# Rotating k before q, and v in 8 KB runs, in an attention and mixture-of-experts kernel

## The chip, the cores and the metric

The kernel runs on one core of one Trainium2 chip, in one launch. Its time is the time on the device, in microseconds (us); the median of several executions counts. One more execution was taken with the hardware profiler, and all stretches and durations below are from that one. The engines of the core are TensorE (PE in the profile; PEld are its weight loads), VectorE (DVE), ScalarE (ACT), GpSimd (POOL), and SyncE (SP), which here only issues DMAs.

## The reference

One transformer layer with the norm behind each half, all in fp32: x is 4 x 1024 x 256, attention has 16 heads of 64 with a rotary embedding and a causal mask, and the second half is a mixture of 16 experts of which each token takes 3.

```
proj = x @ W_in.T + b_in                   # q, k, v: 16 heads x 64 each
q, k = rope(q, sin, cos), rope(k, sin, cos)
att = softmax(mask(q @ k.T / 8)); y = att @ v
x = layernorm(x + y @ W_out.T + b_out)
raw = softmax(x @ gate); top 3 of 16, made to sum to 1
hidden = relu(x @ W1[e] + b1[e]); out = hidden @ W2[e] + b2[e]
x = layernorm(x + sum over the chosen e of gate_e * out_e)

def rope(x):                               # hi: first 32 of a head's 64, lo: last 32
    return concat(lo * cos + hi * sin, hi * cos - lo * sin)
```

## The kernel before, in words

**Tiling.** Attention goes over pairs of heads: 8 pairs for each of 4 sequences, n = 0 to 31. A pair has six slots (k = 0 to 5). Each slot takes one or two chunks of 128 queries, the longest first: chunk 7 (1024 keys by the causal mask), 6, 5, 4, then (3, 2), then (1, 0). A tile has 128 partitions: two heads by 64.

**What happens to a chunk.** `scores` (L254) multiplies q by k on TensorE into PSUM (L275), DVE adds the mask, keeps the row's extreme and writes the result to SBUF (L283), ACT makes the exponential and its row sum (L295). `divide` (L306) takes the reciprocal of the sum on DVE (L309) and multiplies each head's rows by it on POOL (L312). Two slots later `turn` (L321) transposes the divided rows in 32 x 32 blocks on DVE (L333), and `product` (L343) multiplies v by them on TensorE (L357). `close` adds the bias of v on ACT (L370), and `out` (L376) multiplies by the output weights on TensorE (L379) and adds the result to the residual on DVE (L384).

**Projection of the next pair.** In slots 0 to 3 of pair n, `project(n + 1, i, g)` (L193) makes q (i = 0) and k (i = 1) of the next pair: TensorE multiplies one half of 512 positions (L200), ACT adds the bias (L204). i = k // 2 and g = k % 2, so q is made in slots 0 and 1 and k in slots 2 and 3. After the second half, four DMAs copy the result with blocks of 32 partitions swapped into a tile `swp` (L213).

**Rotation.** `rotate` (L215) multiplies the projection by the sine in place, the swapped copy by the cosine, and adds them. The first product waits until the swap DMAs have read the projection. q (in slot 3): the sine on DVE (L217), the cosine (L221) and the sum (L222) on POOL. k (in slot 4): all three on POOL. For the first pair the engines differ. The first scores of a pair need its q and its k rotated: that is the seam between two pairs.

**v.** `values` (L224) projects 256 positions of v for two pairs at a time, in slots 4 and 5: TensorE (L231), ACT (L236), and one DMA to DRAM (L239). `spread` (L245) brings v back, 512 positions at a time, four times over (each time into 32 partitions): partition q holds positions 32 k + q for k = 0 to 15, so a run in DRAM is one position of one pair, 128 floats (L250). It is called in slot 1 (second half) and in slot 4 (first half).

**What sets the order.** TensorE's instructions stand in the order in which the program is written. The others are placed by a scheduler, which keeps the ties made by `after` (an instruction is issued behind the last one of a kind, with no semaphore) and by `late` (SP's DMAs keep program order). `turn` is tied behind the slot's scores, the reciprocals behind the turns. L384 is tied to nothing; the scheduler puts it inside the turns in slot 3 and behind the reciprocals in slots 0, 4 and 5.

**Routing.** Once a sequence is done, its layer norm and the choice of experts run within the next sequence's pairs: the norm in the slot 1 of its second pair, transposes and gate products up to the third pair, the choice (some 60 small DVE operations) in slot 3 of the third, the placing in slot 3 of the fourth, and 24 indirect DMAs issued by POOL that write a table (L641), four each in slots 1 and 3 of the fifth to seventh pairs. After the last pair the experts run (L830, L846, L860), which the change doesn't touch.

Of the kernel before, what the change touches and what calls it, by code (L numbers as in the profile page):

```python
# [37 lines left out]
P = 128  # L38
# [49 lines left out]
def attention(  # L88
# [5 lines left out]
    with ExitStack() as ctx:  # L94
# [98 lines left out]
        def project(n, i, g):  # L193

            b, p = divmod(n, NP)
            if g == 0:
                rot[n, i] = qkp.tile([P, T], FP, tag=f"rot{i}", name=f"rot{i}")
            ps = ps_s.tile([P, 512], FP, tag="s", name="pp")
            for c in range(DC):
                nc.tensor.matmul(  # L200
                    ps, lhsT=wqk[n][:, c, i, :], rhs=xts[b, g][:, c, :],
                    start=(c == 0), stop=(c == DC - 1),
                )
            nc.scalar.activation(  # L204
                rot[n, i][:, ts(g, 512)], ps, AF.Identity,
                bias=(bq_s if i == 0 else bqk[:, 1, :])[:, p : p + 1],
                scale=SCALE if i == 0 else 1.0,
            )
            if g == 1:

                swp = swps[n, i] = qkp.tile([P, T], FP, tag="swp", name="swp")
                for r in range(4):
                    nc.sync.dma_start(out=swp[ts(r, 32), :], in_=rot[n, i][ts(r ^ 1, 32), :])  # L213

        def rotate(n, i):  # L215
            swp, res = swps.pop((n, i)), rot[n, i]
            first = (nc.gpsimd if i and n else nc.vector).tensor_tensor(res, res, sin, ALU.mult)  # L217
            if n and i == 0:
                after(first, "turn" if "turn" in order else "scores")
            eng = nc.vector if n == 0 and i else nc.gpsimd  # L220
            eng.tensor_tensor(swp, swp, cos, ALU.mult)  # L221
            eng.tensor_tensor(res, res, swp, ALU.add)  # L222

        def values(n, cc):  # L224

            b = n // NP
            v = vp.tile([P, 2, 2 * P], FP, tag="v", name="v")
            ps = ps_s.tile([P, 2, 2 * P], FP, tag="s", name="vv")
            for u in range(2):
                for c in range(DC):  # L230
# [4 lines left out]
                    )  # L235
            nc.scalar.copy(v, ps)  # L236
            if cc == 0:
                vds[n // 2] = v_d.tile([T, 2 * P], FP, tag="v_d", name="v_d")
            nc.sync.dma_start(  # L239
                out=vds[n // 2][ts(cc, 2 * P)].rearrange("(u p) d -> p u d", p=P), in_=v  # L240
            )

        vds, vrs = {}, {}

        def spread(n, g):  # L245

            vr = vrs[n, g] = vrp.tile([P, 16, P], FP, tag=f"v{g}", name="vr")
            src = vds[n // 2][ts(g, 512), ts(n % 2, P)].rearrange("(k q) d -> q k d", q=32)
            for a in range(4):
                late(nc.sync.dma_start(out=vr[ts(a, 32)], in_=src))  # L250

# [54 lines left out]
        def divide(n, ends, kind):  # L306
            for qc, rsum in ends:
                rinv = sp.tile([P, 2], FP, tag="rinv", name="rinv")
                after(nc.vector.reciprocal(rinv, rsum), kind)  # L309
                for hh in range(2):  # L310
                    pr = probs[n, qc, hh]
                    router.behind = nc.gpsimd.tensor_scalar(  # L312
                        pr, pr, rinv[:, hh : hh + 1], 1.0, ALU.mult, ALU.mult
# [6 lines left out]

        def turn(n, i, kind):  # L321
            if n not in turned:
# [3 lines left out]
                )  # L326
            for hh in range(2):
                pr = probs.pop((n, i, hh))
                for h, (t, step) in enumerate(zip(turned[n], (7, 3))):
                    n_j = min(4, i + 1 - 4 * h)  # L330
                    if n_j <= 0:
                        continue
                    order["turn"] = router.on_dve = nc.vector.transpose(  # L333
                        t[:, hh, :, ds(i - 4 * h, n_j, step=step), :],
                        pr[:, ds(512 * h, n_j * P)].rearrange(
                            "p (j u q) -> p u j q", u=4, q=32
                        ),
                    )
                    after(order["turn"], kind)

        st = {}

        def product(n, j):  # L343
# [32 lines left out]
        def out(n, h):  # L376
            ps = ps_s.tile([P, 2, D], FP, tag="s", name="oo")
            for v in range(2):
# [29 lines left out]
        with tc.manual_schedule(engines={mybir.EngineType.PE}):  # L408
            for n in range(n_pairs + 2):
# [3 lines left out]
                for k in range(n_slots):  # L413
# [7 lines left out]
                    if k != 2 and one_of(m):  # L421
                        for j in js:
                            product(m, j)
                    if k in (0, 3, 4, 5) and one_of(n - 1 - (k == 0)):
                        out(n - 1 - (k == 0), (k - 3) % 4 if k else 3)
# [624 lines left out]
```

## Time and profile before

| | |
|---|---|
| median of 6 runs | 2107.82 us (2106.53 to 2110.24) |
| the profiled execution | 2109.6 us |
| its span, first to last instruction | 2107.7 us |
| attention, to the last pair's start | 1489.75 us, 31 seams |
| a pair without routing work | 42.4 to 44.0 us |
| a pair with scatters | 53.0 to 56.9 us |
| PE busy | 1751.2 us (83%) |
| POOL busy | 1223.7 us (58%) |
| DVE busy | 1148.9 us (55%) |
| granted TensorE clock | 0.900 of full speed |
| HBM read, written | 193.28 MB, 54.63 MB |

How to read it: the shares of busy time are means over attention and experts. A line of a timeline is: start in us from the span's start, duration, engine, line of the kernel, operation, tiles written and read, sizes, count, and in brackets how long the engine was idle just before and what ended that. `x8` at TensorE counts passes: an fp32 product takes two. "issue" is time in which an engine waited for nothing that the profile shows.

### The profile page before, as it was taken

The numbers are of one execution on the slowest core, as the hardware profiler recorded it, in microseconds if no ns is written. First come the engines' busy times: TensorE is split into PE (matmuls) and PEld (weight loads), VectorE is DVE, ScalarE is ACT, GpSimd is POOL, SyncE is SP. The second block draws the span as 40 slices with busy tenths as digits, with TensorE's granted clock in tenths as the row PEclk, the third lists the DMA queues.
The fourth block names the chain that finished last, engine by engine and source line by source line (L and its number), as shares of the span: only waits on it lengthen the run. The fifth ranks groups of instructions, "written<-read, shape, count | busy, mean of one in ns | idle before, by whom it ended". The sixth has DMA issues, their size and how long they took to land.

```text
span 2107.7 us, 52088 instructions
## 1 busy us (share of the span) xinstructions
PE 1751.2 (83%) x21172; PEld 1194.6 (57%) x21172; DVE 1148.9 (55%) x3453; ACT 724.6 (34%) x1662; POOL 1223.7 (58%) x1037
## 2 busy tenths in 40 slices
PE   7788887898877788887778897877589799999990
PEld 4455554555544455554445565543368588888880
DVE  5566665768755566875555768755445122222224
ACT  4344443444333344443234443333222122222223
POOL 4655565555665565456565564555536677777743
PEclk9889998999988998998889998988689699999995
DMA  6445454563444556354334554333357588888857
GB/s 180 103 122 126 89 117 105 102 174 79 105 88 84 96 122 164 85 120 89 79 86 103 153 117 92 82 72 75 65 212 207 131 227 240 232 237 238 233 129 249
DMA packets 239106, 284.86 MB, mean 135 GB/s; under 512 B 20897, under 2 KB 204321, under 8 KB 230802
## 3 DMA queue, kind: packets, MB, share of 16 engines
q1 hardware_dynamic: 211378, 248.18, 46.3%
q0 software_dynamic: 27344, 33.35, 8.9%
q8 instruction: 166, 2.72, 0.6%
q14 instruction: 74, 0.61, 0.1%
q10 hardware_dynamic: 144, 0.01, 0.0%
HBM read 193.28 MB, written 54.63 MB: 118 GB/s over the span
## 4 chain that ended last, share of the span: by engine, by line
PE 55%; DVE 16%; POOL 14%; issue 8%; DMA 3%; ACT 2%; SPq 1%; another core or an unknown queue 1%; ACTq 0%; POOLq 0%; DVEq 0%
PE y_ps L357 13%; PE ps L830 11%; PE ps L846 11%; PE s L275 10%; PE pp L200 7%; POOL rot L222 4%; DVE p L283 4%; DVE t_first L333 3%; POOL swp L221 3%; POOL p L312 3%; POOL rot L217 3%; DVE t_last L333 3%; PE oo L379 2%; POOL table L641 2%; PE ps L818 1%
## 5 line engine op out<-in xcount | busy, mean ns | idle before, releaser
L312 POOL TENSOR_SCALAR p<-p,rinv 128x512 f32<-128x512 f32 (+7 forms) x512 | 402.2, 800 | 492.5 <-DVE rinv L309 488.5
L295 ACT ACTIVATE p<-p,nmax 128x512 f32<-128x512 f32 (+7 forms) x512 | 392.0, 766 | 651.6 <-DVE nmax L283 592.5
L275 PE MATMUL s<-rot,rot 64*128 64x512 f32 (+3 forms) x1536 | 383.7, 590 | 213.8 <-POOL rot L222 187.0
L283 DVE CUSTOM_DVE_ANT_0 p<-s,zero 128x512 f32<-128x512 f32 x256 | 166.2, 685 | 467.4 <-PE s L275 448.8
L275 PEld LDWEIGHTS s<-rot,rot 64*128 64x128 f32 x1536 | 167.5, 209 | 423.3 <-POOL rot L222 197.3
L333 DVE STREAM_TRANSPOSE t_first<-p 128x512 f32<-128x512 f32 (+3 forms) x512 | 283.9, 583 | 0.0
L200 PE MATMUL pp<-xT,wqk 128*128 128x512 f32 x512 | 254.0, 621 | 20.4 <-DVE nmax L283 14.8
L357 PE MATMUL y_ps<-t_first,vr 32*64 32x160 f32 (+2 forms) x8192 | 233.6, 344 | 14.5 <-issue 12.5
L830 PE MATMUL ps<-xg,w 128*128 128x256 f32 x1008 | 236.8, 388 | 7.4 <-issue 3.7
L860 POOL DMA_INDIRECT sums<-y,ids x126 | 200.8, 1593 | 71.0 <-DVE y L856 36.3
L846 PE MATMUL ps<-w,hid 128*128 128x256 f32 x1008 | 234.7, 385 | 7.6 <-issue 7.2
L835 ACT ACTIVATE hid<-ps,w 128x256 f32<-128x256 f32 x252 | 105.4, 470 | 373.7 <-issue 305.6
L851 DVE TENSOR_TENSOR y<-ps,w 128x512 f32<-128x512 f32 x63 | 43.6, 691 | 344.4 <-PE ps L846 286.3
L221 POOL TENSOR_TENSOR swp<-swp,cos 128x1024 f32<-128x1024 f32 x63 | 150.3, 2385 | 137.6 <-DMA swp<-rot 136.3
L357 PEld LDWEIGHTS y_ps<-t_first,vr 32*64 32x64 f32 x8192 | 175.3, 132 | 84.1 <-issue 56.7
L846 PEld LDWEIGHTS ps<-w,hid 128*128 128x128 f32 x1008 | 193.4, 192 | 38.6 <-issue 13.4
L830 PEld LDWEIGHTS ps<-xg,w 128*128 128x128 f32 x1008 | 191.6, 195 | 34.5 <-issue 6.9
L357 PEld LDWEIGHTS y_ps<-t_last,vr 32*64 32x64 f32 x7424 | 123.0, 147 | 106.1 <-issue 60.4
L357 PE MATMUL y_ps<-t_last,vr 32*64 32x96 f32 (+3 forms) x7424 | 150.9, 274 | 34.0 <-DVE t_last L333 27.3
L200 PEld LDWEIGHTS pp<-xT,wqk 128*128 128x128 f32 x512 | 94.5, 195 | 113.0 <-issue 67.0
L379 PE MATMUL oo<-wo,yT 128*128 128x256 f32 x512 | 153.0, 425 | 2.6 <-ACT yT L370 1.7
L222 POOL TENSOR_TENSOR rot<-rot,swp 128x1024 f32<-128x1024 f32 x63 | 149.6, 2374 | 2.5
(146 smaller groups left out, 1914.8 us busy)
## 6 DMA issues: line engine op xcount, KB each, us to landing
w<-in_wall_dram SPq DMA_DIRECT2D x63, 1154.0 KB
vr<-v_d SPq DMA_DIRECT2D x256, 256.0 KB
swp<-rot SPq DMA_DIRECT2D x256, 128.0 KB
v_d<-v SPq DMA_DIRECT2D x64, 256.0 KB
wqk<-in_w_qk_dram SPq DMA_DIRECT2D x32, 256.0 KB
xT<-in_xT_dram SPq DMA_DIRECT2D x8, 512.0 KB
wv<-in_w_v_dram SPq DMA_DIRECT2D x16, 256.0 KB
wo<-in_w_outT_dram SPq DMA_DIRECT2D x32, 128.0 KB
```

What stands on the lines that cost most here:

```text
L200: nc.tensor.matmul(ps, lhsT=wqk[n][:, c, i, :], rhs=xts[b, g][:, c, :], start=(c == 0), stop=(c == DC - 1),)
L221: eng.tensor_tensor(swp, swp, cos, ALU.mult)
L222: eng.tensor_tensor(res, res, swp, ALU.add)
L275: nc.tensor.matmul(s[:, :n_k], lhsT=q[ts(hh, KD), ts(qc, P)], rhs=k[ts(hh, KD), ds(k0, n_k)], start=True, stop=True,)
L283: order["scores"] = nc.vector.tensor_tensor_reduce(out=probs[n, qc, hh][:, ds(k0, n_k)], in0=s[:, :n_k], in1=mask[:, 512 - n_k :] if last ...
L295: nc.scalar.activation(pr, pr, AF.Exp, bias=m, scale=-1.0, accum_out=rsum[:, hh : hh + 1])
L312: router.behind = nc.gpsimd.tensor_scalar(pr, pr, rinv[:, hh : hh + 1], 1.0, ALU.mult, ALU.mult)
L333: order["turn"] = router.on_dve = nc.vector.transpose(t[:, hh, :, ds(i - 4 * h, n_j, step=step), :], pr[:, ds(512 * h, n_j * P)].rearrange ...
L357: nc.tensor.matmul(st[n][a][ts(hh, KD), ds(32 * j, 32 * (TC - j))], lhsT=vrs[n, h][ts(a, 32), jh * 4 + u, ts(hh, KD)], rhs=t[ts(a, 32), hh ...
L830: nc.tensor.matmul(ps[:, f - f0, :], lhsT=w[:, ds(c * FF + f * P, P)], rhs=xg[:, c, :], start=(c == 0), stop=(c == DC - 1),)
L846: nc.tensor.matmul(ps[:, h, :], lhsT=hid[:, f, ts(h, P)], rhs=w[:, ds(W2_AT + f * D, D)], start=(f == 0), stop=(f == FC - 1),)
L860: s = nc.gpsimd.indirect_dma_start(out=sums[t % 2], out_offset=bass.IndirectOffsetOnAxis(ap=ids[:, h, i : i + 1], axis=0), in_=y[:, h, :], ...
```

## The change

It has three parts.

- **k first.** Slots 0 and 1 now project k, slots 2 and 3 project q (second half first). k is rotated in slot 2 and q in slot 4. Rotations are tied behind the last division (`order["divide"]`) for what POOL does; q's sine product on DVE stays tied behind the last turn.
- **v in DRAM.** The DRAM tile is laid out so that what one partition of `vr` reads is one run of 8 KB. Each `values` stores its two pairs with two DMAs, whose DRAM side has the dimensions 4 x 32 x 256. `product` takes v's rows at other places in the tile.
- **Sums between the turns.** `out` returns what is to be added, and the slot's loop does the sum (was L384) between the turns of the two heads; the reciprocal stands behind them.

```diff
         def project(n, i, g):
             b, p = divmod(n, NP)
-            if g == 0:
+            half_done = (n, i) in rot
+            if not half_done:
                 rot[n, i] = qkp.tile([P, T], FP, tag=f"rot{i}", name=f"rot{i}")
...
-            if g == 1:
+            if half_done:
                 swp = swps[n, i] = qkp.tile([P, T], FP, tag="swp", name="swp")
...
         def rotate(n, i):
             swp, res = swps.pop((n, i)), rot[n, i]
             first = (nc.gpsimd if i and n else nc.vector).tensor_tensor(res, res, sin, ALU.mult)
-            if n and i == 0:
-                after(first, "turn" if "turn" in order else "scores")
+            if n:
+                after(first, "divide" if i else "turn" if "turn" in order else "scores")
             eng = nc.vector if n == 0 and i else nc.gpsimd
-            eng.tensor_tensor(swp, swp, cos, ALU.mult)
+            second = eng.tensor_tensor(swp, swp, cos, ALU.mult)
+            if n:
+                after(second, "divide")
             eng.tensor_tensor(res, res, swp, ALU.add)
...
-            v = vp.tile([P, 2, 2 * P], FP, tag="v", name="v")
+            v = vp.tile([P, 2, 2, P], FP, tag="v", name="v")
...
-            nc.scalar.copy(v, ps)
+            nc.scalar.copy(v.rearrange("p i u d -> p u i d"), ps.rearrange("p u (i d) -> p u i d", i=2))
             if cc == 0:
-                vds[n // 2] = v_d.tile([T, 2 * P], FP, tag="v_d", name="v_d")
-            nc.sync.dma_start(
-                out=vds[n // 2][ts(cc, 2 * P)].rearrange("(u p) d -> p u d", p=P), in_=v
-            )
+                vds[n // 2] = v_d.tile([NG, 2, 32, 2, 4, 2 * P], FP, tag="v_d", name="v_d")
+            for i in range(2):
+                nc.sync.dma_start(
+                    out=vds[n // 2][cc // 2, i, :, cc % 2].rearrange("q k d -> k q d"),
+                    in_=v[:, i],
+                )
...
-            src = vds[n // 2][ts(g, 512), ts(n % 2, P)].rearrange("(k q) d -> q k d", q=32)
             for a in range(4):
-                late(nc.sync.dma_start(out=vr[ts(a, 32)], in_=src))
+                late(nc.sync.dma_start(out=vr[ts(a, 32)], in_=vds[n // 2][g, n % 2].rearrange("q c k d -> q (c k d)")))
...
-                    router.behind = nc.gpsimd.tensor_scalar(
+                    order["divide"] = router.behind = nc.gpsimd.tensor_scalar(
                         pr, pr, rinv[:, hh : hh + 1], 1.0, ALU.mult, ALU.mult
                     )
...
-                            lhsT=vrs[n, h][ts(a, 32), jh * 4 + u, ts(hh, KD)],
+                            lhsT=vrs[n, h][ts(a, 32), jh // 2 * 8 + 2 * u + jh % 2, ts(hh, KD)],
...
-            a = accs[n // NP][:, ds(2 * h, 2), :]
-            nc.vector.tensor_tensor(a, ps, a, ALU.add)
+            return accs[n // NP][:, ds(2 * h, 2), :], ps
...
-                    if one_of(m):
-                        for qc in chunks[kk]:
-                            turn(m, qc, "scores")
-                    divide(n, ends, "turn" if m >= 0 else "scores")
+                    last = "scores"
+                    for hh in range(2):
+                        if one_of(m):
+                            for qc in chunks[kk]:
+                                turn(m, qc, hh, last)
+                            last = "turn"
+                        if hh == 0 and part:
+                            a, ps = part
+                            order["sum"] = after(nc.vector.tensor_tensor(a, ps, a, ALU.add), last)
+                            last = "sum"
+                    divide(n, ends, last)
...
                         if k < 4:
-                            project(n + 1, k // 2, k % 2)
-                        if k in (3, 4):
-                            rotate(n + 1, k - 3)
+                            project(n + 1, *((1, 0), (1, 1), (0, 1), (0, 0))[k])
+                        if k in (2, 4):
+                            rotate(n + 1, int(k == 2))
```

`turn` takes the head as an argument; what it does for one head is unchanged.

More of the change, by code (lines that the diff above doesn't have):

```diff
@@ L319, in attention, with turn @@
         turned = {}
-        def turn(n, i, kind):
+        def turn(n, i, hh, kind):
             if n not in turned:
@@ L326, in turn @@
                 )
[L327 to L339, printed above, removed]
+            pr = probs.pop((n, i, hh))
+            for h, (t, step) in enumerate(zip(turned[n], (7, 3))):
+                n_j = min(4, i + 1 - 4 * h)
+                if n_j <= 0:
+                    continue
+                order["turn"] = router.on_dve = after(nc.vector.transpose(
+                    t[:, hh, :, ds(i - 4 * h, n_j, step=step), :],
+                    pr[:, ds(512 * h, n_j * P)].rearrange("p (j u q) -> p u j q", u=4, q=32),
+                ), kind)
         st = {}
@@ L423, in attention @@
                             product(m, j)
+                    part = None
                     if k in (0, 3, 4, 5) and one_of(n - 1 - (k == 0)):
-                        out(n - 1 - (k == 0), (k - 3) % 4 if k else 3)
+                        part = out(n - 1 - (k == 0), (k - 3) % 4 if k else 3)
                     m, kk = divmod(n * n_slots + k - 2, n_slots)
-                    if one_of(m):
-                        for qc in chunks[kk]:
-                            turn(m, qc, "scores")
-                    divide(n, ends, "turn" if m >= 0 else "scores")
+                    last = "scores"
[9 more added lines that the diff above has]
+                    divide(n, ends, last)
                     if k == 0 and one_of(n + 2) and n % 2 == 0:
```

## The prediction

> **What bounds the kernel now.** I read the chain of waits first, then the list of waits, then the timelines of one head pair. The list says whom the chain's largest engine waits for:
>
> ```profile
> PE 55%; DVE 16%; POOL 14%; issue 8%; DMA 3%; ACT 2%; SPq 1%; another core or an unknown queue 1%; ACTq 0%; POOLq 0%; DVEq 0%
> ```
> ```profile
> PE s L275 <- POOL rot L222: 187.0, 28, 15.5
> ```
>
> TensorE leads, and its largest wait by far (187.0 us, 28 times) is for the rotated k: the first score product of a pair (L275) waits for POOL's last sum of the rotation (L222). That is once a pair, at the seam between two pairs. TensorE's timeline of the pair from 277.45 to 320.68 us shows it:
>
> ```profile
> 277.45 3.78 PE L275 MATMUL s<-rot,rot 64*128 64x512 f32 x8 [5.61 <-POOL rot L222]
> ...
> 313.18 1.89 PE L231 MATMUL vv<-wv,xT 128*128 128x256 f32 x8
> 320.68 1.22 PE L275 MATMUL s<-rot,rot 64*128 64x512 f32 x2 [5.61 <-POOL rot L222]
> ```
>
> Its work is done at 315.07 and the next pair starts at 320.68. (The eight score matmuls after the wait take 3.78 us; at 285.91 the same eight take 1.77.) POOL's timeline, from the third slot of that pair:
>
> ```profile
> 298.62 2.36 POOL L221 TENSOR_TENSOR swp<-swp,cos 128x1024 f32<-128x1024 f32 x1 [5.14 <-DMA swp<-rot]
> 301.38 1.78 POOL L312 TENSOR_SCALAR p<-p,rinv 128x768 f32<-128x768 f32 x2 [0.39 <-DVE rinv L309]
> 305.90 2.47 POOL L312 TENSOR_SCALAR p<-p,rinv 128x640 f32<-128x640 f32 x2 [2.74 <-DVE rinv L309]
> 308.34 2.37 POOL L222 TENSOR_TENSOR rot<-rot,swp 128x1024 f32<-128x1024 f32 x1
> 311.12 2.48 POOL L312 TENSOR_SCALAR p<-p,rinv 128x512 f32<-128x512 f32 x4 [0.41 <-DVE rinv L309]
> 313.57 2.35 POOL L217 TENSOR_TENSOR rot<-rot,sin 128x1024 f32<-128x1024 f32 x1
> 315.88 2.34 POOL L221 TENSOR_TENSOR swp<-swp,cos 128x1024 f32<-128x1024 f32 x1
> 318.29 2.34 POOL L222 TENSOR_TENSOR rot<-rot,swp 128x1024 f32<-128x1024 f32 x1
> ```
>
> q's cosine product (298.62) falls into an idle stretch, q's sum (308.34) into the middle, and all three operations of k come last, 7.07 us after the slot's divisions. Between 301.38 and 320.64 POOL idles only 2.74 + 0.41 us. So the pair's length is TensorE's and DVE's way to the reciprocal of slot 2 (301.28), and from there POOL's work.
>
> **Moving k ahead of q.** In the changed program POOL's order in a pair is: divisions of slot 2 (768 wide), k's three operations, divisions of slot 3 (640), of slot 4 (512 and 384), then q's cosine product and sum. DVE's product of q with the sine (L217) moves from slot 3 to behind the reciprocals of slot 4. TensorE's and ACT's orders stay, k and q only change places. From 301.38 on:
>
> - divisions of 768: 1.78 (row above)
> - k's three: 7.07 (313.57 to 320.64). Their transfers are k's now and issued as q's were; those landed before 298.62, so nothing is late
> - divisions of 640: 1.57 when undisturbed, by the first pair:
>
> ```profile
> 45.52 1.57 POOL L312 TENSOR_SCALAR p<-p,rinv 128x640 f32<-128x640 f32 x2 [2.36 <-DVE rinv L309]
> ```
>
> - what DVE's sine product takes from POOL. These rows show that the two engines exclude each other when DVE reads two SBUF operands:
>
> ```profile
> 305.73 1.20 DVE L217 TENSOR_TENSOR rot<-rot,sin 128x1024 f32<-128x1024 f32 x1
> ```
> ```profile
> 489.13 2.39 POOL L221 TENSOR_TENSOR swp<-swp,cos 128x1024 f32<-128x1024 f32 x1
> ```
> ```profile
> 489.36 2.31 DVE L583 TENSOR_TENSOR hot<-hot,rank 128x128 f32<-128x128 f32 x1
> ```
>
> The divisions of 640 beside the product at 305.73 took 2.47 for 1.57, so POOL lost 0.90; a DVE operation of 0.25 us (L583 at 494.87) took 2.31, ending with POOL's at 491.5. The product now comes at about 310.9 (slot 4's reciprocals end at 311.09 today; the second swap's packets end at 310.4), inside the divisions of 640 (from 310.2), and POOL has no idle time left to absorb it. I take 1.05, between 0.90 and the full 1.20. Bounds: 0, if it met a gap, and 1.75, the longest product of this line beside a division (436.39).
> - divisions of slot 4: 2.48
> - q's two: 4.76 (315.88 to 320.64)
>
> Sum 18.71, so q is ready at 320.09 instead of 320.64: **-0.55 us a pair**. POOL loses the 2.36 that lay in the idle stretch and fills 3.15 of waiting instead. Before slot 2 nothing moves: TensorE fills slots 0 and 1 without a wait. 31 seams by kind:
>
> - 13 plain ones (waits of 5.6, first one 8.4): 13 x -0.55 = -7.2.
> - 9 with table scatters in slots 1 and 3 (waits of 10.2, last one 15.5). Today from 627.01 (divisions of 768) to 650.86: 23.85. Slot 3's four scatters with their gaps (0.16 + 1.05 + 0.30 + 0.98 + 0.30 + 0.97 + 0.30 + 0.97 = 5.03) now follow the divisions of 640: 18.71 + 5.03 = 23.74. 9 x -0.1 = -1.0.
> - 3 with a layer norm in slot 1 (waits of 2.88). There the first swap landed only at 433.81 behind the stores of x. Now k's three start there: 433.81 + 7.07 + 1.57 + 1.05 + 2.48 + 4.76 = 450.74 for 452.46: -1.7. TensorE's own end is 449.63, so its wait falls to 1.1. After a wait of 2.88 the eight score matmuls took 3.78, after one of 1.70 (at 548.91) 1.99; up to 1.8 more to gain, I take half. 3 x -2.6 = -7.8.
> - 3 with the routing choice on DVE in slots 3 to 5. Today the seam has no wait (TensorE ends and starts at 502.47) since most of k was done while DVE was late: after slot 4's reciprocals (496.56) POOL needs only 2.81 + 2.38. Then it will need 2.48 + 1.05 + 4.76 = 8.29 from 496.68, 504.97. The reciprocals themselves come earlier: the product leaves (1.12), and k's three end near 486.4, so fewer DVE operations wait for POOL (L567, L582, L583 lost 1.2 + 0.8 + 2.1), but eight more small ones of some 0.2 stand ahead. I take 1.4 of a possible 0 to 3. 504.97 - 1.4 - 502.47 = +1.1. 3 x +1.1 = +3.3.
> - 3 with the placing in slot 3 (wait 1.70): 541.64 + 8.29 = 549.93, less 0.8 for the product that left, against 548.85: +0.3 x 3 = +0.9.
>
> **v in runs of 8 KB.** A load of vr is now 32 runs of 8 KB instead of 512 of 512 B. In the packet records a group of four loads has 2048 packets, from 310.3 to 315.8. I cost the gain at nothing: that v is first read in the next pair, 14 us later, and vr waits are 4.4 us in the whole run. The stores of v become two for one, each 1 KB packets as now (46 ns each, 22 GB/s an engine). Their 64 extra issues (0.37 to 0.43 us) stand in SP's queue behind the swaps and the vr loads of their slot; what follows (wqk, x or wv) is wanted 15 us later. Only at the start is something queued: four extra issues ahead of the load of acc, whose sum (L174) POOL does at 32.15 ahead of all its divisions. And the stores' outermost dimension is now 4, not 128. If such a store kept to a quarter of the engines, its 256 packets a slot would take 64 x 46 ns = 2.9 us; four of them from 19.3 end at 31.1, where today they end at 25.0. acc would come about 3 later, and the first turn of the second slot, which waits for divisions that end at 38.9, about 2. Bounds 0 and +2, I take **+1**. In the loop 2.9 us for each store still end before the next pair reads. The Trainium skill (DMA: Bandwidth & Descriptors, section "Why a DMA increments its semaphore by 16 and not by 1") has a rule against this layout: a DMA runs on the largest number of engines up to 16 that divides both outermost dimensions, here 4. No row here shows such a store; by the rule the term is +2, by today's spread 0.
>
> **Sums between the turns.** L384 moves between the two heads' turns and so ahead of the reciprocal: 0.65 later for POOL's divisions in slots 0, 4 and 5, about 1.4 in slot 0 where it waits for the output product (284.1). Cover: slot 0 leaves POOL 4.3 us of idle time; slot 4's divisions start after 312.8 now, its reciprocals end near 310.8; slot 5's divisions follow q. Without that cover it would cost 0.65. Cost 0.
>
> **Sum.** -7.2 - 1.0 - 7.8 + 3.3 + 0.9 + 1.0 = **-10.8 us**. The profiled execution took 2109.6 (span 2107.7), 1.8 above the median 2107.82: 2098.8 for it, **2097** for the median.
>
> **Rivals.**
>
> A, slower: POOL is saturated from slot 2 to the seam, and DVE's sine product holds it 1.75 instead of 1.05. For: 1.75 was seen; today's order has 3.15 of idle to absorb it, the new one none. Against: the product itself is 1.20, the rest of that 1.75 was DVE waiting. 31 x 0.7 = 21.7, so +11: **2119**. It decides from 0.35 more per seam.
>
> B, same: the gain on the plain seams is real, but the choice and placing seams lose their slack (reciprocals not earlier: +1.4 and +0.8 more, x 3 = 6.6) and the layer-norm seams gain no clock (2.7 less): -10.8 + 9.3 = -1.5, **2106**.
>
> C, faster still: the product costs POOL nothing (it meets a hand-over, or the ports are shared): 31 x 1.05 = 32.6, -43: **2064**.
>
> D: the 512 B loads starve TensorE's instruction supply and 8 KB ends that. For: in the scatter pairs 128 output matmuls of slot 1 take 8.4 us (612.79 to 621.2) for 3.5 in plain ones, "issue" gaps. Against: the vr packets end at 612.1 there, and POOL's scatters run just then. 9 x 4.9 = 44: 2053.
>
> **How the numbers follow.** Forecast 0.54 (its own range 2085 to 2103: -0.3 and +0.15 on 31 seams about, and the bounds 0 and 2 at the start), A 0.22, B 0.14, C 0.07, D 0.03. What this kernel's measurement can tell is 0.2%, 4.2 us. Faster: forecast, C, D, 0.64. Same: B, with a little of both sides, 0.15. Slower: A, 0.21. The range to 2 in 10 outside: **2076 to 2119**.
>
> **What would show it.** In a plain pair POOL from the divisions of 768 to q's sum without idle, 18.7 us; the wait of L275 for the rotation (then q's) 5.0, not 5.6; scatter seams at 10.1; layer-norm seams near 1; the choice pairs with a new wait of about 1. The sine product at 1.2 to 1.5 beside a division of 640 stretched to 2.6. Wrong if the divisions of 768 start earlier or later in the pair than 23.9 us after its first score, if POOL idles between them and the seam, or if the first pair starts its second slot 5 us late.

## The result and the profile after

The changed kernel took 2097.55 us (median of 20 runs, 2089.96 to 2101.56), the kernel before 2108.89 in the runs beside it: a ratio of 0.9947, 95% interval 0.9933 to 0.9961. Its profiled execution has a span of 2100.7 us for 2107.7.

POOL's timeline of the same pair as before, which now starts at 278.93 (columns: start, duration, then the instructions; in brackets the idle time ahead and what ended it):

```profile
302.82 1.79 POOL L317 TENSOR_SCALAR p<-p,rinv 128x768 f32<-128x768 f32 x2 [7.88 <-DVE rinv L314]
304.57 2.37 POOL L218 TENSOR_TENSOR rot<-rot,sin 128x1024 f32<-128x1024 f32 x1
306.89 2.36 POOL L222 TENSOR_TENSOR swp<-swp,cos 128x1024 f32<-128x1024 f32 x1
309.34 2.38 POOL L225 TENSOR_TENSOR rot<-rot,swp 128x1024 f32<-128x1024 f32 x1
311.69 5.07 POOL L317 TENSOR_SCALAR p<-p,rinv 128x640 f32<-128x640 f32 x6
316.73 2.34 POOL L222 TENSOR_TENSOR swp<-swp,cos 128x1024 f32<-128x1024 f32 x1
319.14 2.34 POOL L225 TENSOR_TENSOR rot<-rot,swp 128x1024 f32<-128x1024 f32 x1
```

From the divisions of 768 to q's sum POOL does not idle: 302.82 to 321.48 is 18.66 us. The row with six divisions holds those of slots 3 and 4 together: 5.07 us, which is 1.57 + 2.48 and 1.02 more, the price of DVE's product with the sine. The new thing to see is the first bracket: 7.88 us of idle time ahead of this chain. By the records of the DMA packets, the copies into k's `swp` had ended at 299.60, so k's data were there 3.2 us before the chain began. TensorE's timeline at the end of this pair:

```profile
314.54 1.89 PE L234 MATMUL vv<-wv,xT 128*128 128x256 f32 x8
321.54 1.23 PE L280 MATMUL s<-rot,rot 64*128 64x512 f32 x2 [5.11 <-POOL rot L225]
```

The wait at the seam was 5.61 and is 5.11. The list of waits of the whole run (total, times, longest) shows more seams with a wait, since three pairs with the routing choice have one now:

```profile
PE s L280 <- POOL rot L225: 191.9, 31, 16.2
```

Two places became slower. One is the start. The transfers of its first 45 us in 40 slices (each digit the busy share of the 16 DMA engines in tenths), in the kernel before and in the changed one, and POOL's first sum in both:

```profile
DMA  0289899999209829986616479999998300793000
```
```profile
DMA  0279999997005955962222223479997999769821
```
```profile
32.15 4.54 POOL L174 TENSOR_TENSOR acc<-acc,bo 128x2048 f32<-128x2048 f32 x1 [8.71 <-DMA acc<-in_x_dram]
```
```profile
40.73 4.50 POOL L174 TENSOR_TENSOR acc<-acc,bo 128x2048 f32<-128x2048 f32 x1 [16.83 <-DMA acc<-in_x_dram]
```

In the stretch of 2s about a quarter of the engines' time was busy, and POOL's first sum starts at 40.73 (32.15 before). The other is the tail. TensorE's, DVE's and POOL's timelines of the last pair (its start is 1475.56):

```profile
1512.96 0.47 PE L358 MATMUL y_ps<-t_last,vr 32*64 32x64 f32 x4 [0.94 <-issue]
...
1514.57 2.07 PE L380 MATMUL oo<-wo,yT 128*128 128x256 f32 x4
```
```profile
1507.06 0.40 DVE L337 STREAM_TRANSPOSE t_last<-p 128x256 f32<-128x256 f32 x1
1520.28 0.69 DVE L436 TENSOR_TENSOR acc<-oo,acc 128x512 f32<-128x512 f32 x1 [12.82 <-PE s L280]
...
1521.84 0.18 DVE L314 RECIPROCAL rinv<-rsum 128x2 f32<-128x2 f32 x2
```
```profile
1517.00 0.95 POOL L816 DMA_INDIRECT x<-x_a,ids  x1 [0.30 <-issue]
1522.06 2.48 POOL L317 TENSOR_SCALAR p<-p,rinv 128x512 f32<-128x512 f32 x4 [4.12 <-DVE rinv L314]
```

The sum between the two heads' turns (L436) waits for an output product on TensorE, which stands behind attention products that run in small bursts while POOL issues the gathers. (The bracket names the score products behind it, L280. Three signals from TensorE reached DVE almost together, from 1520.26 to 1520.38, and the first in program order is the output product's; the end of its row, 1516.64, is modelled.) So the second head's turns and the reciprocals come late, and POOL, done with its gathers, waits 4.12 us for them. In the kernel before, whose last pair starts at 1489.75, the reciprocals of this slot were done 33.9 us after the pair's start, ahead of the wait, and POOL went from the gathers to the divisions at once:

```profile
1523.61 0.18 DVE L309 RECIPROCAL rinv<-rsum 128x2 f32<-128x2 f32 x2
1535.52 0.69 DVE L384 TENSOR_TENSOR acc<-oo,acc 128x512 f32<-128x512 f32 x1 [11.73 <-PE s L275]
```
```profile
1533.27 2.48 POOL L312 TENSOR_SCALAR p<-p,rinv 128x512 f32<-128x512 f32 x4
```

Where the 7.0 us between the two profiles came from, by the terms of the prediction; the second pair of profiles is from two more runs of both kernels on one other chip (spans 2113.7 and 2100.3). A pair is counted from its first score product to that of the next:

| term | predicted | first profiles | second |
|---|---|---|---|
| first pair | +1 and a plain seam, -0.55 | +7.2 | +6.6 |
| 12 other plain pairs | -6.6 | -13.9 | -12.4 |
| 3 with a layer norm | -7.8 | -8.2 | -7.8 |
| 3 with the choice | +3.3 | +4.0 | +4.7 |
| 3 with the placing | +0.9 | +2.1 | +4.4 |
| 9 with table scatters | -1.0 | -6.0 | -13.6 |
| last pair to the first expert product | 0 | +7.0 | +4.8 |
| ahead of the first score, and experts | 0 | +0.7 | +0.1 |
| span | -10.8 | -7.0 | -13.4 |

In the first profile of the kernel before, the 12 plain pairs took 42.2 to 45.1 us each and the scatter pairs 49.0 to 56.9; the ranges in the table ahead of the prediction are too narrow.

### The profile page after: what moved, and what is told of

The parts are those of the page before. It is cut to its first block, busy times and chain, and to the rows that moved or that the text cites. A ratio compares the mean times of both kernels' runs of the same rounds, so it can differ in the third digit from the quotient of the medians.

```text
span 2100.7 us, 52116 instructions
## 1 busy us (share of the span) xinstructions
PE 1740.4 (83%) x21172; PEld 1189.0 (57%) x21172; DVE 1157.5 (55%) x3453; ACT 723.6 (34%) x1662; POOL 1224.5 (58%) x1037
## 3 DMA queue, kind: packets, MB, share of 16 engines
q1 hardware_dynamic: 87986, 248.18, 42.4%
## 4 chain that ended last, share of the span: by engine, by line
PE 53%; POOL 17%; DVE 10%; issue 9%; DMA 5%; ACT 3%; SPq 2%; another core or an unknown queue 0%; ACTq 0%; POOLq 0%; DVEq 0%
PE y_ps L358 11%; PE ps L839 11%; PE ps L855 10%; PE s L280 10%; PE pp L201 6%; POOL p L317 5%; POOL swp L222 4%; POOL rot L225 4%; PE oo L380 3%; DMA swp<-rot 2%; DVE p L288 2%; DVE t_first L337 2%; POOL table L650 2%; SPq L214 2%; ACT p L300 2%
## 5 line engine op out<-in xcount | busy, mean ns | idle before, releaser
L280 PE MATMUL s<-rot,rot 64*128 64x512 f32 (+3 forms) x1536 | 378.2, 596 | 208.5 <-POOL rot L225 191.9
L280 PEld LDWEIGHTS s<-rot,rot 64*128 64x128 f32 x1536 | 167.2, 211 | 410.5 <-POOL rot L225 203.4
L337 DVE STREAM_TRANSPOSE t_first<-p 128x512 f32<-128x512 f32 (+3 forms) x512 | 289.1, 588 | 6.9 <-POOL p L317 6.9
L839 PE MATMUL ps<-xg,w 128*128 128x256 f32 x1008 | 236.2, 385 | 17.3 <-issue 12.7
L358 PE MATMUL y_ps<-t_first,vr 32*64 32x160 f32 (+3 forms) x8192 | 229.6, 342 | 13.9 <-issue 11.2
L855 PE MATMUL ps<-w,hid 128*128 128x256 f32 x1008 | 230.4, 381 | 3.3 <-issue 3.3
```

The costliest lines, as they stand in the source:

```text
L280: nc.tensor.matmul(s[:, :n_k], lhsT=q[ts(hh, KD), ts(qc, P)], rhs=k[ts(hh, KD), ds(k0, n_k)], start=True, stop=True,)
L337: order["turn"] = router.on_dve = after(nc.vector.transpose(t[:, hh, :, ds(i - 4 * h, n_j, step=step), :], pr[:, ds(512 * h, n_j * P)].rea ...
L358: nc.tensor.matmul(st[n][a][ts(hh, KD), ds(32 * j, 32 * (TC - j))], lhsT=vrs[n, h][ts(a, 32), jh // 2 * 8 + 2 * u + jh % 2, ts(hh, KD)], r ...
L839: nc.tensor.matmul(ps[:, f - f0, :], lhsT=w[:, ds(c * FF + f * P, P)], rhs=xg[:, c, :], start=(c == 0), stop=(c == DC - 1),)
L855: nc.tensor.matmul(ps[:, h, :], lhsT=hid[:, f, ts(h, P)], rhs=w[:, ds(W2_AT + f * D, D)], start=(f == 0), stop=(f == FC - 1),)
```

## The experiments

The kernel before took 2108 to 2118 us on most chips used and 2035 on one; each ratio is against its runs on the same chip. The columns in us are read from the profile of each run: the first pair, the mean of the 12 other plain pairs, in these POOL's way from the divisions of 768 to the last sum of a rotation, the mean of the 9 scatter pairs, and the time from the start of the last pair to the first expert product. A star marks the faster chip, where the scatter pairs take some 6 us less in the kernels run there.

| kernel | ratio (interval) | first | plain | way | scatter | tail |
|---|---|---|---|---|---|---|
| before, again | 0.9988 (0.9978 to 0.9998) | 36.8 | 43.1 | 19.0 | 53.9 | 70.1 |
| changed, again | 0.9925 (0.9912 to 0.9939) | 43.5 | 42.1 | 18.6 | 52.4 | 74.9 |
| order of k and q alone * | 0.9947 (0.9930 to 0.9963) | 36.3 | 42.5 | 18.6 | 47.8 | 64.1 |
| v's layout alone * | 0.9984 (0.9975 to 0.9993) | 44.4 | 42.9 | 19.1 | 47.2 | 63.3 |
| sums between the turns alone * | 1.0067 (1.0050 to 1.0083) | 36.7 | 44.0 | 19.8 | 47.8 | 68.5 |
| changed, old sums from the last pair on * | 0.9954 (0.9938 to 0.9971) | 43.4 | 42.1 | 18.6 | 47.3 | 64.4 |
| changed, old sums everywhere | 0.9935 (0.9917 to 0.9953) | 44.3 | 42.1 | 18.6 | 53.2 | 68.8 |
| changed, one store, 2 KB runs | 0.9888 (0.9872 to 0.9904) | 37.2 | 42.2 | 18.6 | 52.3 | 71.8 |
| changed, two stores, 2 KB runs | 0.9910 (0.9880 to 0.9940) | 37.4 | 42.3 | 18.6 | 52.6 | 74.3 |
| one store, old sums from the last pair on | 0.9883 (0.9868 to 0.9898) | 36.7 | 42.1 | 18.6 | 53.0 | 67.0 |
| changed, without q's sine product | 0.9741 (0.9725 to 0.9758) | 42.4 | 41.0 | 17.6 | 51.4 | 72.8 |
| one store, old sums from the last pair on, rotations earlier on POOL | 0.9230 (0.9203 to 0.9256) | 36.6 | 37.4 | | 46.0 | 66.7 |

The first line says what two measurements of one program can differ by: 0.12%. The changed kernel gave 0.9947 and 0.9925, 0.22% apart.

**The three parts alone.** Each is the kernel before with one part of the change's diff. The order of k and q:

```diff
-                            project(n + 1, k // 2, k % 2)
-                        if k in (3, 4):
-                            rotate(n + 1, k - 3)
+                            project(n + 1, *((1, 0), (1, 1), (0, 1), (0, 0))[k])
+                        if k in (2, 4):
+                            rotate(n + 1, int(k == 2))
```

> The kernel before with only the order of k and q changed (k projected and rotated first, its three operations on POOL behind the divisions of 768). If the gains at the seams come from this part alone: POOL's way from the divisions of 768 to the rotation's last sum falls from 19.26 to 18.6 in a plain pair, the start and the tail stay as in the kernel before (first pair 36.4 us, last score of the first pair 31 to the first expert product as before), and the time falls by 5.4 (plain chains) + 8.2 (layer norm) + 3.8 (scatter) - 4.0 (choice) - 0.7 (placing) = 12.7, to about 2095. Rival: the other 9 us, by which the divisions of 768 started earlier in the changed kernel's pairs (0.73 in a plain pair), come from this part too: about 2086. Rival of the prediction's rival A: no gain, 2106 or more.

Measured: ratio 0.9947, which is 10.8 us of 2035; POOL's way 18.62. The theory's 12.7 lies inside the interval (7.5 to 14.2 us); the rival's 22 does not, so the earlier divisions of 768 are not all from this part. Beside the two profiles of the kernel before, which are from other chips, the plain pairs fell from 43.1 and 43.3 to 42.5 us and the choice pairs rose from 49.6 and 49.9 to 50.6, about as the prediction had it.

v's layout alone (the hunks of `values`, `spread` and the weights' index in `product`):

```diff
-                vds[n // 2] = v_d.tile([T, 2 * P], FP, tag="v_d", name="v_d")
+                vds[n // 2] = v_d.tile([NG, 2, 32, 2, 4, 2 * P], FP, tag="v_d", name="v_d")
```

> The kernel before with only v's layout in DRAM changed (runs of 8 KB for the loads, two stores for one with an outermost dimension of 4). If the lost start comes from this part: the stores of the start run on four engines until about 32 us, acc's sum starts at 40 instead of 32, the first pair takes 43 to 44 us instead of 36.4, and the time rises by 7, to about 2115, with the seams unchanged. Rival: the fewer packets (116,000 for 239,000) are what brought the divisions of 768 forward by 0.73 us a plain pair, 9 us in all: then the start's 7 is paid back and the time is about 2106, with POOL's way at the seam at 19.26 still. Second rival: the start is not from this part, and the time is 2108.

Measured: the first pair took 44.4 and acc's sum started at 39.63, so the lost start is this part's:

```profile
39.63 4.50 POOL L174 TENSOR_TENSOR acc<-acc,bo 128x2048 f32<-128x2048 f32 x1 [17.02 <-DMA acc<-in_x_dram]
```

And yet the time fell, by 3.3 us (1.4 to 5.1). The loop pays the start back, which is the rival's outcome. The divisions of 768 start 23.76 us into a plain pair there, for 24.07 and 24.25 in the profiles of the kernel before on other chips: 0.3 to 0.5 earlier, where the rival had 0.73.

The sums alone (the hunks of `turn`, `out` and the slot loop):

```diff
+                        if hh == 0 and part:
+                            a, ps = part
+                            order["sum"] = after(nc.vector.tensor_tensor(a, ps, a, ALU.add), last)
```

> The kernel before with only the output sums moved between the two heads' turns. If the lost tail comes from this part: the last pair's sums wait for the output products, which stand behind products that starve while POOL issues the gathers, the second head's turns and the divisions wait for the sums, and from the start of the last pair to the first expert product it takes 75 us instead of 68: about 2115, seams unchanged. Rival: the sums cost nothing and the tail's 7 us come from elsewhere (phase of the gathers, k before q): 2108. Second rival: they bring the divisions of 768 forward as well (9 us): 2106.

Measured: 1.0067, or 13.6 us slower, twice what the theory gave. The tail is there (68.5 for 63 to 64 with the other parts). The rest is in the plain pairs, 44.0 us for 43.1 and 43.3 in the kernel before on other chips. POOL's timeline of the pair that starts at 279.67 there:

```profile
308.10 2.46 POOL L312 TENSOR_SCALAR p<-p,rinv 128x640 f32<-128x640 f32 x2 [2.74 <-DVE rinv L309]
310.53 2.37 POOL L222 TENSOR_TENSOR rot<-rot,swp 128x1024 f32<-128x1024 f32 x1
313.91 2.48 POOL L312 TENSOR_SCALAR p<-p,rinv 128x512 f32<-128x512 f32 x4 [1.01 <-DVE rinv L309]
```

POOL waits 1.01 us for the reciprocals of slot 4, where it waited 0.41 in the kernel before, and k's three operations, the seam, stand behind these divisions. That 0.6 is the sum ahead of the reciprocal (0.65). With k rotated first, the reciprocals of slot 4 have time and the wait is gone.

**The sums in the changed kernel.** First put back from the last pair on alone, then everywhere:

```diff
-                        if hh == 0 and part:
+                        if hh == int(n >= n_pairs - 1) and part:
```

> The changed kernel, with the output sums behind both heads' turns again from the last pair on alone (some 10 sums). If they made the tail 7 us longer: from the start of the last pair to the first expert product 68 to 69 us instead of 75.4, and about 2091 for 2097.6. Rival: no change in the tail, 2097.

Measured: a tail of 64.4 (the changed kernel was not profiled on that chip; the sums alone gave 68.5 there, kernels with the old order 63 to 64). The ratio, 0.9954, shows no gain against the changed kernel's 0.9925 to 0.9947: inconclusive for the total.

> The kernel before once more, for its profile beside those of the single parts, which ran on a faster chip (2035 for 2108). Expected there: ratio 1.000; the first pair 36.4 us, plain pairs with POOL's divisions of 768 at 24.2 and POOL's way from there to the rotation's last sum of 19.05 to 19.26; from the start of the last pair to the first expert product 64 us. If the profile of the part with v alone (plain pairs 42.87, scatter pairs 47.2) stands below its, v's layout gains in the loop what it loses at the start.

> The changed kernel once more, beside its parts: ratio 0.9947 again (10.8 of 2035). The parts alone gave 0.9947 for the order of k and q, 0.9984 for v's layout and 1.0067 for the sums, -10.8 - 3.3 + 13.6 = -0.5 us together: so if the parts only added, 0.9998. Theory: they do not add, since the sums' delay of the reciprocals in slot 4 falls on POOL's way to the seam only while k is rotated last. Last pair to first expert product 68 to 70.

> The changed kernel with the sums behind both heads' turns as before (k first and v's layout alone). Theory: the sums cost their 5 us of the tail and nothing else: plain pairs and POOL's way (18.6) as in the changed kernel, last pair to first expert product 64, and a ratio of 0.992 (5 us under the changed kernel). If the two parts add: -10.8 - 3.3 = -14.1, 0.993. Rival: the sums pay in the loop, by turns that come earlier: 0.995 or more.

Measured, all three on one chip: the kernel before gave 0.9988. The chip was not the faster one, so the tails that were expected (64, and 68 to 70) do not apply, with 70.1 and 74.9 measured, and a profile of the kernel before beside that of v's layout is missing. The parts do not add, since the changed kernel keeps 0.9925 and not 0.9998; the parts were measured on the faster chip, so the size of the difference is less sure than its sign. K first and v's layout, without the sums, do add: 0.9935 for 0.993. Without the sums between the turns the tail falls from 74.9 to 68.8, by 6.1 us where some 5 were expected, and the plain pairs stay at 42.1. But the ratio does not fall: the nine scatter pairs together took 478.7 for 471.8. Whether the sums did that can't be told. Two kernels below differ from the last pair on alone, and their scatter pairs took 471.1 and 477.3.

**The start.** v_d with k ahead of q, so that a store is one transfer of 128 rows. The loads, which then read runs of 2 KB, and the weights' index in `product` follow (not shown):

```diff
-                vds[n // 2] = v_d.tile([NG, 2, 32, 2, 4, 2 * P], FP, tag="v_d", name="v_d")
+                vds[n // 2] = v_d.tile([NG, 2, 4, 32, 2, 2 * P], FP, tag="v_d", name="v_d")
...
+            nc.sync.dma_start(
+                out=vds[n // 2][cc // 2, :, :, :, cc % 2].rearrange("i k q d -> (k q) i d"),
+                in_=v.rearrange("p i u d -> p i (u d)"),
+            )
```

> The changed kernel with v_d laid out so that a store is one transfer with an outermost dimension of 128 (k before q; the loads take 2 KB runs, four for each partition, instead of one of 8 KB). Theory: the start's loss is that of stores on four engines with four more issues: acc's sum at 32 instead of 40 us, first pair 36.4 instead of 43.5, and if 2 KB runs serve the loop as well as 8 KB, 7 us under the changed kernel, ratio 0.991. Rival: the start is late because the loads of 8 KB pass acc's packets: the first pair stays at 40 or more. Second rival: the loop needs the 8 KB: the start is regained and 4 to 10 us lost in the pairs, 0.993 to 0.996.

> The kernel with runs of 2 KB, but two stores for one as in the changed kernel, each now with an outermost dimension of 128. It splits the start's 6.3 to 7.2 us: if the stores' spread over engines is the cause, the stores' packets run on 16 engines, acc's load is issued at 27.7 as in the changed kernel (23.9 before), acc's sum starts at 33 to 36 instead of 40.7, and the first pair takes 37 to 40 us, since only the four later issues are left. If those issues are the cause, the first pair stays at 42 or more. In the loop no difference to one store: ratio 0.989 to 0.990.

Measured: first pairs of 37.2 (one store) and 37.4 (two stores, issued as often as in the changed kernel). So the four extra issues are worth 0.2 us of the first pair. The other 6 belong to the stores' spread over engines and to the loads' shorter runs together: both kernels change both, so the rival with the 8 KB loads is not refused by them. The stretch from 20 to 28 us, where the loads of vr have not begun, of the changed kernel and of the one with two stores (busy time and count of PE, PEld, DVE, ACT and POOL, granted clock, DMA share, GB/s):

```profile
20.00:28.00 8.00, 3.96 (x15) 2.62 (x16) 5.74 (x3) 1.17 (x2) 3.83 (x2) 0.82 0.27 84
```
```profile
20.00:28.00 8.00, 3.88 (x17) 2.77 (x17) 5.73 (x3) 1.18 (x2) 4.21 (x2) 0.84 0.64 166
```

0.27 of 16 engines is 4.3, with 0.64 it is 10 (the load of acc begins within this stretch there). The loop is as fast with runs of 2 KB as with 8 KB (plain pairs 42.2 and 42.3), and the whole gains 0.4%, 0.9925 to 0.9888 on one chip. With two stores the interval is wider and holds both.

**The sums' tail on top of it:** the kernel with one store and the old order of the sums from the last pair on.

> The kernel with stores of one transfer and runs of 2 KB, and besides the sums behind both heads' turns from the last pair on alone. If the sums cost the tail 5 to 6 us (74.9 with them, 68.8 without) and this is all that they cost: last pair to first expert product 66 to 68 instead of 71.8, and 5 us under that kernel's 0.9888, a ratio of 0.986. Rival: the gathers' phase sets the tail and not the sums: 0.989.

Measured: the tail is 67.0 for 71.8, the total 0.9883 for 0.9888. The 4.8 us are seen in the profiles; in the total, taken on two chips, they are not.

**The price of DVE's product.** From the second pair on q's product with the sine is left out:

```diff
-            first = (nc.gpsimd if i and n else nc.vector).tensor_tensor(res, res, sin, ALU.mult)
+            first = None
+            if i or not n:
+                first = (nc.gpsimd if i and n else nc.vector).tensor_tensor(res, res, sin, ALU.mult)
```

> The changed kernel without q's product with the sine on DVE from the second pair on (a part of the computation is left out). The prediction's price: the product holds POOL for 1.05 us in every pair. If so, POOL's way from the divisions of 768 to q's sum falls from 18.6 to 17.6 in plain pairs, and the divisions of 640 or of 512 lie at 1.57 and 2.48 in every pair; 31 seams by 1.0, some 28 us under the changed kernel, a ratio of about 0.980. Rival C of the prediction: the product costs POOL nothing, 18.6 stays, ratio 0.993 to 0.995.

POOL's timeline of the pair that starts at 272.40 there:

```profile
295.97 1.79 POOL L319 TENSOR_SCALAR p<-p,rinv 128x768 f32<-128x768 f32 x2 [7.88 <-DVE rinv L316]
...
304.83 4.02 POOL L319 TENSOR_SCALAR p<-p,rinv 128x640 f32<-128x640 f32 x6
```

The six divisions take 4.02 us for 5.07, and POOL's way is 17.62 for 18.58. So the product costs POOL 0.96 to 1.05 us, on the path of every seam; rival C falls. The ratio, 0.9741, is lower than the 0.980 expected: against the changed kernel's second profile the plain pairs became 1.1 us shorter, but the placing pairs 2.9. What these gained beyond the product's price is not explained.

**The idle time ahead of the chain.** The 7.88 us of the first fence, with k's swap done earlier, asked for one more kernel: the one with one store and the old sums from the last pair on ("the last text" below is its expectation), with k's three operations behind the divisions and scatters of slot 1, and q's two ahead of the divisions of slot 4.

```diff
-            eng.tensor_tensor(res, res, swp, ALU.add)
+            order["rotate"] = eng.tensor_tensor(res, res, swp, ALU.add)
...
+                    if n:
+                        after(order["divide"], "rotate")
...
+                    if k == 4 and one_of(n + 1):
+                        rotate(n + 1, 0)
                     divide(n, ends, last)
...
-                        if k in (2, 4):
-                            rotate(n + 1, int(k == 2))
...
+                    if k == 1 and one_of(n + 1):
+                        rotate(n + 1, 1)
```

The tie to `order["rotate"]` keeps each division behind the last rotation ahead of it.

> The kernel of the last text and besides: k's three operations behind the divisions of slot 1 (and its table scatters) instead of slot 2, and q's two ahead of the divisions of slot 4 instead of behind. Reason: in the changed kernel POOL idles 6 to 8 us ahead of the divisions of 768 while k's swap has landed some 4 us earlier. Theory: in a plain pair k's three start near 20 us in the pair, the divisions of 768 move from 23.9 to 27, q's sum ends at 39.4 instead of 42.6, the wait at the seam falls from 5.0 to about 2 and the first eight scores run in 2.0 to 3.0 instead of 3.8: 3 to 4 a plain pair; in a scatter pair q's sum at 46 instead of 53.9, 6 to 8; together 80 to 100 us, a ratio of 0.94 to 0.95. Rival: the turns of slot 4 wait for the later divisions of 768, TensorE's own end slides with them and less than 30 us is left. Second rival, for pairs with a layer norm or a choice: k's swap lands at 26 behind other stores, and POOL stands ahead of the divisions: slower there by 2 to 5.

Measured: 1949.66 us for 2117.11, ratio 0.923 (0.9203 to 0.9256): more than expected. POOL's and TensorE's timelines of the pair that starts at 250.35:

```profile
268.75 2.36 POOL L218 TENSOR_TENSOR rot<-rot,sin 128x1024 f32<-128x1024 f32 x1 [4.99 <-DMA swp<-rot]
...
275.85 3.33 POOL L316 TENSOR_SCALAR p<-p,rinv 128x768 f32<-128x768 f32 x4
281.16 3.43 POOL L222 TENSOR_TENSOR swp<-swp,cos 128x1024 f32<-128x1024 f32 x1 [1.98 <-DMA swp<-rot]
284.66 2.35 POOL L225 TENSOR_TENSOR rot<-rot,swp 128x1024 f32<-128x1024 f32 x1
```
```profile
287.06 1.99 PE L279 MATMUL s<-rot,rot 64*128 64x512 f32 x8 [1.80 <-POOL rot L225]
```

k's operations start 18.4 us into the pair, the divisions of 768 at 25.5 (23.9 before), q's sum ends at 36.7 instead of 42.6, the seam's wait is 1.80, and the first eight scores run in 1.99 us for 3.8, at a granted clock of 1.00 for 0.50. Against the same kernel without this edit the plain pairs gained 4.7 us each, the scatter pairs 7.1, choice pairs 4.7 and placing pairs 4.2, 146 us together; pairs with a layer norm gained nothing (42.9 for 42.8), because there the first swap lands late. The kernel makes two moves, k into the idle time and q ahead of the divisions of slot 4 (2.48 us), and their shares were not taken apart.

## Why the prediction was right

The total was right, 2097 for 2097.55, and its main step with it. That it fits to within 1 us is luck: the start and the tail were missed by some 7 us each, and the plain and the scatter pairs made up for them with 7 and 5 us more than was forecast.

- **POOL's chain at the plain seams.** 18.71 predicted, 18.66 in the pair it was worked out for and 18.61 in the mean; the divisions of 768 started 23.89 us into that pair, where 23.9 was the condition. The order of k and q alone gave -10.8 us; the seam terms without the start add to -11.8. But in the mean of the 12 plain pairs POOL's way fell by only 0.42, from 19.03, which is 5.0 of their 13.9 us. The other 8.9 come from ahead of the chain: the divisions of 768 start 23.51 us into a pair instead of 24.25, where the prediction had "Before slot 2 nothing moves". TensorE's first scores of slot 2 start 18.18 and 17.91 us into a plain pair in the two profiles of the kernel before, 18.03 with the order of k and q alone, 17.73 with v's layout alone (both on the faster chip) and 17.69 in the changed kernel; from there to the divisions of 768 it is 6.07 and 6.16, 5.83, 6.03 and 5.82. So the layout brought TensorE forward by 0.2 to 0.5 us, and the order of k and q what follows by some 0.2 to 0.3.
- **The sine product at 1.05.** 0.96 to 1.05 by taking it away. Rival A's 1.75 is refused. The Trainium skill (SBUF — State Buffer, section "SBUF: two separate sides") has the pair of ports that DVE and POOL share as an exclusive lock for a whole instruction, for a DVE operation with two SBUF inputs; the 5.07 against 4.02 us agree.
- **The start, +1.** The mechanism was weighed and its size missed. The stores did take the time of about four engines (0.27 of 16), as the bound assumed: packets of 1 KB went at 59 to 95 a us from 20 to 28, where four engines at 46 ns a packet give 87. The step that failed is "acc would come about 3 later". If acc's packets are spread over all 16 engines, a quarter of them queues behind the stores, and then shares those engines with the 8 KB packets of the vr loads, which the prediction left out: from 32 to 40 us the DMA share was 0.97, where the kernel before had 0.63, and from 35 to 39 packets of 1 KB went at 29 to 39 a us. The last of them came at 39.5 (31.2 before), acc's sum 8.6 later, and the first pair took 7.2 more. An estimate from these counts: the 219 packets of 1 KB from 34.0 on took 5.5 us, and 2.5 at 87 a us, so some 3 us are the sharing and some 5 the queue behind the stores. The records of the packets name no engine, and no run takes the two apart. The rule of the Trainium skill (DMA: Bandwidth & Descriptors, section "Why a DMA increments its semaphore by 16 and not by 1"), the largest number up to 16 that divides both outermost dimensions, agrees with the 0.27; the +2 that the prediction drew from it was too small for the same reason.
- **Sums between the turns at 0.** For the loop the cover that was named held, and only with k first: the sums alone cost 0.7 to 0.9 a plain pair against the kernel before on other chips, and the prediction had 0.65 for the case without cover. What failed is that the cover was looked for in the pairs alone. In the last pair no rotation and no next score hides the reciprocals, and TensorE's output product is late there: +4.8 to +7.0.
- **8 KB loads gain nothing.** Wrong by a small amount for each pair. What rival D rests on is there: in plain pairs the "issue" gaps ahead of the attention products are 0.22 to 0.29 us a pair in all four profiles of kernels with 512 B loads, 0.02 to 0.09 with runs of 2 or 8 KB. That TensorE's instruction supply is the reason is not shown. Its price of 4.9 for scatter pairs is refused: the gaps there were 1.0 before and 1.1 after. With the layout the plain pairs went from 42.5 (order of k and q alone) to 42.1. What else the layout gave in v's kernel alone, where the loop made good about 11 us, stays open: the kernel before was not profiled on that chip.
- **Layer-norm pairs, -7.8.** The sum is right, its way was not. The wait stayed (3.1 instead of 1.1) and TensorE's own end came 3 us earlier: in the kernel before, q's cosine product stood on POOL waiting for the swap, and the divisions of 768 behind it started only 28.9 us into the pair; now they come first, at 23.1. The prediction took TensorE's end as fixed.
- **Choice and placing.** +3.3 and +0.9 for +4.0 to +4.7 and +2.1 to +4.4. The new wait in the choice pairs is 3.4 and not 1, but TensorE's end is 2 us earlier there.
- **Scatter pairs, -1.0.** The seam's wait (median of the nine) fell from 10.19 to 9.97, where 10.1 was predicted. The -6.0 and -13.6 of the pairs are not explained: these pairs differ by 6 us between kernels that are the same there.

## What to carry to other kernels

A chain that runs without idle time is worth reading from its first instruction: what ends the idle time ahead of it may be a position in a queue and not the data. Moving work there, with q's rotation moved ahead of two divisions as well, gave 6.6%, where the change described here gave 0.5%. Parts of a change need not add: a delay that costs nothing in the loop behind one order costs some 9 us behind another, and cover has to be looked for in the last round of a loop too. A store whose outermost dimension is small can delay what is queued behind it, above all at the start, where nothing hides it.

## What the runs showed of the hardware

- With stores of an outermost dimension of 4 the transfers filled the time of 4.3 engines from 20 to 28 us, with 128 rows that of 10 (the load of acc begins in that stretch), for the same packets of 1 KB.
- DVE's product of two SBUF operands, 1.2 us long, took 0.96 to 1.05 us from POOL's divisions, whichever of them it met.
- Eight passes of score products behind a wait of 5.11 us at the seam ran at a granted clock of 0.50 in 3.8 us, behind a wait of 1.80 at 1.00 in 1.99.
- One program took 2035 us on one chip and 2108 to 2118 on others. Without the last kernel and the one without the sine product, the scatter pairs took 47 to 48 us there for 52 to 54, with "issue" gaps ahead of the attention products of 0.04 to 0.07 us a pair for 1.0 to 1.6 (none in v's kernel); the changed kernel's plain pairs took 42.1 to 42.2 on the others, and 42.1 on that chip with the old sums from the last pair on.
